# Score matmuls of a causal attention: one pass per head from 64-row operands kept in DRAM by head, in place of four 32-row tiles side by side; constants set up later

## The chip, the cores and the metric

The kernel runs on one core of one Trainium2 chip. The metric is the time of one execution on the device in microseconds (us); the figure for the kernel before is the median of three runs. Durations of single operations come from one profiled execution, whose own time is given beside its span.

## The reference

Two transformer layers over an input of 4 sequences x 2048 tokens x 256 channels, in fp32, each layer an attention and a feed-forward part with a layer norm before and a residual sum behind. Cut to what matters here:

```python
x = x + L0_attn(layernorm(x))      # one head of 64, causal over the 2048 tokens
x = x + L0_ffn(layernorm(x))       # operands rounded to fp8, one 256x256 matmul, bias
x = x + L1_attn(layernorm(x))      # 16 heads of 16, rotary embedding, causal over 2048 tokens
x = x + L1_ffn(layernorm(x))       # token shift mix, sigmoid gate, relu squared

# L1_attn: Q, K, V = x W^T split into 16 heads, rope on Q and K, then per head
scores = Q @ K.T / sqrt(16)
attn = softmax(where(causal, scores, -inf))
out = (attn @ V) @ W_O.T
```

## The kernel before, in words

The tokens are cut into 16 blocks of 512 (`BLK`): 4 sequences (b) with 4 blocks (qb) each. `order` lists them. A block's layer 0 (`l0_attention`, `l0_ffn`), its Q, K, V of layer 1 (`l1_qkv`), its layer-1 attention and what follows (`l1_out`, `l1_ffn`) are separate streams of work.

**A planner sets the order.** Nothing is emitted when the Python code meets it. `op` (L77) and `pe` (L493) record an operation with an engine, an estimated occupancy, the buffers it reads and writes and a stream; `Plan.run` (L118) then lists all operations in the order of a simulated schedule: among the ready ones on each engine it takes the earliest by due time (`key`, L1316), charges TensorE `SWITCH` (L63) for going between its modes (F whole array, R 32-row tiles, C 32-column tiles), and gives buffers of the classes in `CLASSES` (L367) to slots. Each engine executes its list strictly in that order. SP issues the DMAs, also in one order.

**fp32 from fp32r.** Scores are made from an fp32r high part and an fp32r remainder of Q and of K (`split`, L683: a cast on DVE, L686, and a subtraction on GpSimd, L687). All four products (high x high, low x low, high x low, low x high) are summed.

**Q and K of layer 1.** `l1_qkv` projects, applies rope (L862, L866 on GpSimd), splits, and `move` (L691 and L692) copies rows with SP's DMAs into tiles of 128 rows: `k1` and two Q tiles, Qa and Qb, for each of four groups of four heads. A head has 32 rows in each: 8 + 8 high, 8 + 8 low; in Qb high and low change places. So each head's scores are two 32-row matmuls, Qa x K and Qb x K, and four heads lie side by side in the array's four row tiles. Each block takes 48 such moves in layer 1. K and V of all blocks of a sequence stay in SBUF.

**Two phases per group of heads.** Phase D (`d_units`, L906) makes scores with queries on the partitions, only to find each row's maximum: a unit is four heads x 128 queries x up to 512 keys; `d_mm` (L924), on the diagonal block four small matmuls per head that add the causal mask (`d_mask`, L930), then DVE's `reduce_max` (L937). When a group's units are done, `shifts` (L941) negates the maximum (L948), splits it into three bf16 parts on GpSimd (L661 to L664), transposes them on TensorE (L675), and ScalarE copies the rows into M (L679). Phase E (`e_units`, L956) makes scores with keys on the partitions: a unit is four heads x 128 keys x up to 512 queries. `e_shift` (L986) adds the shift by a bf16 matmul of ones with M, `e_mm` (L974) twice, on the diagonal `e_mask` (L980); ScalarE takes the exponent (L993); `values` (L1057) multiplies it with V in four 32-column tiles, fp32.

**The burst.** `burst` (L999) emits the matmuls of two heads of an E unit and two heads of a D unit alternately, so that all four row tiles have work; a second burst has the heads the other way round. If PSUM banks are free in the plan, the first burst also does the shift of the second one's E heads (`ahead`). Each head's scores take one PSUM bank; there are eight. D runs about one group and `LEAD` = 2 units ahead of E (`target`, L1186). Behind every E unit come its values.

**The start.** ScalarE's queue issues loads of constants; GpSimd makes masks, and 48 small DMAs (L461 to L463) copy identity and masks into four-fold form; behind them stand wo0's memset and, on ScalarE's queue, the loads of wo0, bf and wf (L468 to L475); DVE clamps and rounds wf to fp8 values (L476 to L482) before its first layer norm. Block i's x goes to DRAM after layer 0 (`keep_x`) and comes back for Q, K, V and for the end (`fetch_x`).

Layer 0 has one head: its scores are whole-array passes already, 128 rows (64 high, 64 low), L739 and L740 for the maximum, L769 and L770 for the exponent, with the masks L742 and L772.

## Time and profile before

| what | value |
|---|---|
| runs | 2978.33 us median (2966.24 to 2981.45) |
| profiled execution, its own time | 2972.05 us |
| its span, first to last instruction | 2970.2 us |
| granted TensorE clock, mean | 0.971 |
| maxima of phase D, L937 (DVE) | 1425.2 us busy, 2560 of them |
| exponents of phase E, L993 (ScalarE) | 1238.1 us busy, 2560 of them |
| D scores L924, E scores L974 (TensorE) | 944.9 and 874.4 us busy, 5120 of each |
| values L1057 (TensorE) | 613.5 us busy, 5120 of them |
| DMA | 148.54 MB; SP's queue 142.68 MB in 14.6% of 16 engines' time |

How to read it: busy times of lines are unions, and tiles that run side by side are counted in several lines, so they do not add up to the engine's. PE is TensorE's matmuls, PEld its weight loads, which overlap them. A matmul's recorded duration holds its pipeline's latency; what it costs in a stream is the distance from its start to the next start. A timeline line gives the start, the duration from first to last of the merged instructions, engine, line, operation, output and inputs, count, and in brackets how long the engine idled before it and what released it. The lines of the busy times by stretch give the stretch, its length, the busy time of PE, PEld, DVE, ACT and POOL, the granted clock, DMA's busy share and GB/s.

### The profile page before, as it was taken

To read this page: it belongs to the slowest core of one execution; us is meant where nothing else is said; L and a number is where in the kernel's file an instruction comes from. 1 tells how busy PE (TensorE), PEld (TensorE's weight loads), DVE (VectorE), ACT (ScalarE), POOL (GpSimd) and SP (SyncE) were. 2 spreads that over 40 slices of the span, in tenths; PEclk is the share of its full clock that TensorE was granted. 3 is DMA by queue.
4 is the path that set the end of the run, shared out by engine and by line. 5 is a ranking of instruction groups with operands and counts; after the bars stand their busy time and mean duration, and the time that the engine had idled before them with its cause. 6 is when DMAs were issued, how large, how long until landed. Compare 5 with 4: busy or idle time off the path is not lost.

```text
span 2970.2 us, 74535 instructions
## 1 busy us (share of the span) xinstructions
PE 2753.7 (93%) x30485; PEld 1440.9 (49%) x30560; DVE 1935.8 (65%) x3941; ACT 1681.1 (57%) x3441; POOL 721.8 (24%) x983
## 2 busy tenths in 40 slices
PE   2598999999999999999999999999999999999987
PEld 1355545544445555544444555544454565444443
DVE  1256667777663668767773676868685476778771
ACT  1244556656666455655657455565656656566665
POOL 4432313212131132301321141321040323120000
PEclk9699999999999999999999999999999999999998
DMA  2312111210120121211121112121020112010000
GB/s 61 102 54 78 54 37 62 86 40 26 54 69 34 37 80 54 73 37 33 39 77 40 57 55 71 48 68 41 9 79 25 56 59 87 27 43 9 12 12 15
DMA packets 114200, 148.54 MB, mean 50 GB/s; under 512 B 20225, under 2 KB 66754, under 8 KB 113858
## 3 DMA queue, kind: packets, MB, share of 16 engines
q1 hardware_dynamic: 110848, 142.68, 14.6%
q8 instruction: 240, 3.93, 0.5%
q14 instruction: 102, 0.84, 0.1%
q10 hardware_dynamic: 1474, 0.69, 0.1%
q0 software_dynamic: 1536, 0.40, 0.1%
HBM read 63.61 MB, written 16.78 MB: 27 GB/s over the span
## 4 chain that ended last, share of the span: by engine, by line
PE 72%; DVE 11%; POOL 5%; issue 4%; ACT 4%; SPq 2%; DMA 2%; POOLq 0%; ACTq 0%; DVEq 0%
PE ps L1057 16%; PE ps L924 10%; PE ps L623 8%; PE ps L986 8%; PE ps L974 7%; DVE mx L937 6%; PE ps L630 5%; PE ps L781 4%; PE ps L980 3%; PE ps L930 2%; ACT p L993 2%; PE ps L604 2%; SPq L692 2%; PE ps L739 1%; PE ps L769 1%
## 5 line engine op out<-in xcount | busy, mean ns | idle before, releaser
L937 DVE TENSOR_REDUCE mx<-ps 128x1 f32<-128x512 f32 (+3 forms) x2560 | 1425.2, 603 | 615.2 <-PE ps L924 232.4
L993 ACT ACTIVATE p<-ps 128x512 f32<-128x512 f32 (+3 forms) x2560 | 1238.1, 532 | 848.8 <-PE ps L974 340.0
L924 PE MATMUL ps<-k,q 32*128 32x512 f32 (+3 forms) x5120 | 944.9, 422 | 68.7 <-DVE mx L937 40.4
L974 PE MATMUL ps<-q,k 32*128 32x512 f32 (+3 forms) x5120 | 874.4, 433 | 0.3 <-issue 0.3
L1057 PE MATMUL ps<-p,v 128*32 128x512 f32 (+3 forms) x5120 | 613.5, 545 | 1.7 <-issue 1.1
L924 PEld LDWEIGHTS ps<-k,q 32*128 32x128 f32 x5120 | 435.9, 186 | 191.3 <-DVE mx L937 98.0
L986 PE MATMUL ps<-m,ones_b 32*128 32x512 bf16 (+3 forms) x2560 | 455.6, 354 | 14.7 <-ACT p L993 4.8
L974 PEld LDWEIGHTS ps<-q,k 32*128 32x128 f32 x5120 | 419.8, 187 | 80.2 <-issue 77.0
L986 PEld LDWEIGHTS <-ones_b 32*128 32x128 bf16 x2560 | 119.2, 91 | 515.0 <-issue 501.9
L623 PE MATMUL ps<-wb,W 128*128 128x256 f32 x768 | 189.6, 391 | 2.2 <-DVE mx L937 1.6
L661 POOL CAST mp<-sm 128x16 bf16<-128x16 f32 x64 | 17.3, 271 | 704.7 <-DVE sm L948 602.2
L930 PE MATMUL ps<-maskC,identC 32*128 32x32 bf16 (+3 forms) x4096 | 179.9, 201 | 0.0
L1057 PEld LDWEIGHTS ps<-p,v 128*32 128x32 f32 x5120 | 106.0, 108 | 146.7 <-issue 107.9
L980 PE MATMUL ps<-maskTC,identC 32*128 32x32 bf16 (+3 forms) x4096 | 168.3, 197 | 0.0
L623 PEld LDWEIGHTS ps<-wb,W 128*128 128x128 f32 x768 | 139.8, 191 | 32.5 <-issue 8.3
L553 POOL TENSOR_SCALAR sm<-sm 128x4 f32<-128x4 f32 x64 | 14.8, 231 | 576.4 <-DVE sm L547 519.6
L781 PE MATMUL ps<-p,v 128*65 128x512 f32 (+3 forms) x320 | 151.6, 561 | 2.8 <-ACT p L776 2.7
L575 ACT ACTIVATE w<-x,sm 128x256 f32<-128x256 f32 x192 | 105.6, 597 | 60.7 <-DVE sm L560 44.8
L930 PEld LDWEIGHTS <-identC 32*128 32x128 bf16 x4096 | 127.9, 95 | 22.4 <-issue 15.7
L687 POOL TENSOR_TENSOR r<-w,r 128x512 fp32r<-128x512 f32 x80 | 103.5, 1295 | 125.9 <-DVE r L686 77.2
L604 PE MATMUL ps<-ident,w 128*128 128x128 f32 x384 | 66.4, 301 | 72.9 <-ACT w L575 72.1
L630 PE MATMUL ps<-W,wa 128*128 128x512 f32 x256 | 125.4, 617 | 0.7 <-ACT W L608 0.7
(116 smaller groups left out, 2845.6 us busy)
## 6 DMA issues: line engine op xcount, KB each, us to landing
q<-r SPq DMA_DIRECT2D x512, 64.0 KB, 1.9
x<-mid SPq DMA_DIRECT2D x64, 256.0 KB, 3.1
k<-r SPq DMA_DIRECT2D x256, 64.0 KB, 1.9
x<-in_x SPq DMA_DIRECT2D x32, 256.0 KB, 3.8
wa<-in_wqk1T SPq DMA_DIRECT2D x32, 256.0 KB, 2.8
q<-r SPq DMA_DIRECT2D x64, 128.0 KB, 2.4
mid<-x SPq DMA_DIRECT2D x32, 256.0 KB, 2.0
out_y<-x SPq DMA_DIRECT2D x32, 256.0 KB, 2.2
```

The lines of the kernel that those rows point to most:

```text
L604: nc.tensor.transpose(p[:, c0 : c0 + P], T_(src)[:, u * C + k * P : u * C + (k + 1) * P], idn)
L623: nc.tensor.matmul(dst, lhsT[:, k, t * P : (t + 1) * P], w[:, k, :], start=(k == 0), stop=(k == CK - 1),)
L630: nc.tensor.matmul(dst, w[:, k, c0 : c0 + P], xT[:, k, :], start=(k == 0), stop=(k == CK - 1))
L781: nc.tensor.matmul(T_(acc)[: D0 + 1, c0:], T_(V_)[:, kt % TT, :], T_(p)[:, c0:], start=(kt == 0), stop=(kt == nkt - 1),)
L924: nc.tensor.matmul(T_(u.banks[h])[:, : u.w], T_(Q)[ROWS[h], u.t * P : (u.t + 1) * P], T_(u.K)[ROWS[h], : u.w], start=(z == 0), stop=(z == ...
L930: nc.tensor.matmul(T_(u.banks[h])[:, u.w - P + c * 32 : u.w], identC[ROWS[h], c, :], maskC[ROWS[h], c, c * 32 :], start=False, stop=(c == 3),)
L937: op("DVE", dve(u.w), lambda h=h: nc.vector.reduce_max(T_(u.mx)[:, u.t * HG + h, u.kb : u.kb + 1], T_(u.banks[h])[:, : u.w], axis=AX.X), r ...
L974: nc.tensor.matmul(T_(u.banks[h])[:, u.c0 :], T_(u.K)[ROWS[h], k * P : (k + 1) * P], T_(Q)[ROWS[h], u.c0 :], start=False, stop=stop,)
L980: nc.tensor.matmul(T_(u.banks[h])[:, u.c0 : u.c0 + (c + 1) * 32], identC[ROWS[h], c, :], maskTC[ROWS[h], c, : (c + 1) * 32], start=False, ...
L986: nc.tensor.matmul(T_(u.banks[h])[:, u.c0 :], ones_b[ROWS[h], :], T_(u.M)[ROWS[h], u.c0 :], start=start, stop=stop,)
L993: op("ACT", act(u.w), lambda h=h: nc.scalar.activation(T_(u.ps[h])[:, u.c0 :], T_(u.banks[h])[:, u.c0 :], AF.Exp, scale=DK**-0.5), r=[u.ba ...
L1057: nc.tensor.matmul(T_(acc)[h * 32 : (h + 1) * 32, u.c0 :], T_(u.V)[:, u.kt % TT, v0 : v0 + 32], T_(u.ps[h])[:, u.c0 :], start=(u.kt == 0), ...
```

## The change

Q and K of layer 1 are kept in DRAM by head. A head has 64 rows: for K high, high, low, low (16 each), for Q high, low, low, high, so that one matmul of 64 rows sums all four products. `l1_qkv` stores the rope output with 16 DMAs of 256 KB per block; V goes to DRAM through a staging tile. `fetch` brings 64 x 512 operands back: four Q per group, four K per group and key block for D (class `kd`, six slots), four for E (`ke0` to `ke3`, two slots each), and V's part for E.

For E, the operands have 12 more rows (76): in `ke` ones at three rows of the head and zeros elsewhere, set once; in Q the three parts of the shift of all four heads, copied in by one DMA per head after `shifts`. So E is one matmul per head that includes the shift, and on the diagonal one more, of identity and mask, 128 columns (`causal`). D is one matmul per head; its diagonal mask moves to DVE, whose maximum becomes a `tensor_tensor_reduce` with the mask added (`row_max`), in layer 0 too. D and E heads alternate (`both`); values come for two E units at a time (`PAIR`). E starts at the diagonal block. The context goes through DRAM before the output projection.

Constants: the 48 copies are gone; the loads come first; the rest of the memsets, the ones of `ke` and wf's rounding are planned into layer 0 of block 0. Block 0's x is used directly for its Q, K, V. The planner's costs change too.

```diff
+QR = 4 * DK
+SR = 3 * HG
...
-PIPE = {"R": 330.0, "C": 213.0, "F": 200.0}
+PIPE = {"R": 185.0, "C": 213.0, "F": 200.0}
 SLACK_OPT = 250.0
 
-SWITCH = {"RC": 140.0, "RF": 211.0, "CR": 113.0, "CF": 217.0, "FR": 94.0, "FC": 120.0,
-          "RR": -60.0, "FF": 15.0, "CC": 30.0}
+SWITCH = {"RC": 122.0, "RF": 118.0, "CR": 145.0, "CF": 143.0, "FR": 120.0, "FC": 130.0,
+          "RR": -70.0, "FF": 0.0, "CC": 30.0}
...
-                eng_free[e] = s + 60.0
+                eng_free[e] = s + 500.0
...
+OFF_FETCH = -15000.0
+PAIR = 2
...
-        "k1": (16, [P, BLK], F32R),
-        "v1": (4, [P, TT, NH * VW + SLOT_PAD], F32),
-        "q": (10, [P, BLK], F32R),
+
+        "kd": (6, [QR, BLK], F32R),
+        **{f"ke{h}": (2, [QR + SR, BLK], F32R) for h in range(HG)},
+        "q": (10, [QR + SR, BLK], F32R),
+        "v1": (5, [P, TT * HG * VW + SLOT_PAD], F32),
+        "vs": (1, [P, NG, TT * HG * VW], F32),
...
-        "mp1": (2, [P, TT, P], BF16),
-        "m": (2, [P, BLK], BF16),
-        "p": (7, [P, BLK], F32),
+        "mp1": (1, [P, TT, QR + SR], BF16),
+        "m": (1, [P, BLK], F32R),
+        "p": (12, [P, BLK], F32),
...
+    expo = const.tile([P, TT], F32, name="expo")
+    nc.gpsimd.memset(expo, -0.5)
+    warm = const.tile([P, TT], F32, name="warm")
+    nc.scalar.activation(warm, expo, AF.Exp)
+    wo0 = const.tile([D0 + 1, C + 1], F32, name="wo0")
+    nc.gpsimd.memset(wo0, 0.0)
     wqk0 = load([P, CK, 2 * D0], kpn(wqk0T), "wqk0", q=nc.scalar)
     bqk = load([P, 1], bqk0, "bqk", q=nc.scalar)
     wv0 = load([P, CK, D0], kpn(wv0T), "wv0", q=nc.scalar)
     bv_bc = load([P, D0], bv0.partition_broadcast(P), "bv_bc", q=nc.scalar)
+
+    nc.gpsimd.memset(wo0[D0 : D0 + 1, C : C + 1], 1.0)
+    nc.scalar.dma_start(wo0[:D0, :C], wo0T)
+    nc.scalar.dma_start(wo0[D0 : D0 + 1, :C], bo0)
+    wf16 = const.tile([P, CK, C], F16, name="wf16")
+    wcf, wce, wcm = (t[:, :2, :].rearrange("p k n -> p (k n)") for t in tiles["x1"][:3])
+    nc.scalar.dma_start(wcf.rearrange("p (k n) -> p k n", k=CK), kpn(wfT))
+    bf_bc = load([P, C], bf.partition_broadcast(P), "bf_bc", q=nc.scalar)
+    mu_sb = load([P, 2, CK], mu, "mu_sb", q=nc.scalar)
...
+    dmask = const.tile([P, BLK], BF16, name="dmask")
+    nc.gpsimd.memset(dmask, 0.0)
+    nc.gpsimd.affine_select(
+        out=dmask[:, BLK - P :], in_=dmask[:, BLK - P :], pattern=[[-1, P]],
+        compare_op=ALU.is_ge, fill=NEG, base=0, channel_multiplier=1,
+    )
...
-    identC = const.tile([P, 4, P], BF16, name="identC")
-    maskC = const.tile([P, 4, P], BF16, name="maskC")
-    maskTC = const.tile([P, 4, P], BF16, name="maskTC")
-    for h in range(HG):
-        for c in range(4):
-            r, s = slice(h * 32, h * 32 + 32), slice(c * 32, c * 32 + 32)
-            nc.gpsimd.dma_start(identC[r, c, :], ident_b[s, :])
-            nc.gpsimd.dma_start(maskC[r, c, :], mask_b[s, :])
-            nc.gpsimd.dma_start(maskTC[r, c, :], maskT_b[s, :])
...
+    def ready_l0():
+        for t in tiles["v0"]:
+            nc.gpsimd.memset(t[:, :, D0 : D0 + 1], 1.0)
+        for t in tiles["mp0"]:
+            nc.gpsimd.memset(t, 0.0)
+
+    def ready_l1():
+        for t in tiles["mp1"]:
+            nc.gpsimd.memset(t, 0.0)
+        for t in tiles["v1"]:
+            nc.gpsimd.memset(t[:, TT * HG * VW :], 1.0)
+        for t in tiles["vs"]:
+            nc.gpsimd.memset(t, 1.0)
+
+    rows_h = tiles["cx"][0]
+
+    def ready_ke(h):
+
+        r = rows_h[QR : QR + SR, h * P : (h + 1) * P]
+        nc.gpsimd.memset(r, 1.0)
+        nc.gpsimd.affine_select(
+            out=r, in_=r, pattern=[[0, P]], compare_op=ALU.is_ge, fill=0.0,
+            base=-3 * h, channel_multiplier=1,
+        )
+        nc.gpsimd.affine_select(
+            out=r, in_=r, pattern=[[0, P]], compare_op=ALU.is_ge, fill=0.0,
+            base=3 * h + 2, channel_multiplier=-1,
+        )
+        for t in tiles[f"ke{h}"]:
+            nc.gpsimd.tensor_copy(
+                t[QR : QR + SR, :].rearrange("p (a n) -> p a n", n=P),
+                r[:, None, :].to_broadcast([SR, BLK // P, P]),
+            )
+
+    def ready_wf():
+
+
+        nc.vector.tensor_scalar(wcf, wcf, 448.0, -448.0, ALU.min, ALU.max)
+        nc.vector.tensor_scalar(
+            wce.bitcast(I32), wcf.bitcast(I32), 0x7F800000, None, ALU.bitwise_and
+        )
+        nc.vector.tensor_scalar(wcm, wce, 2.0**-6, 1.5 * 2.0**20, ALU.max, ALU.mult)
+        nc.vector.tensor_tensor(wcf, wcf, wcm, ALU.add)
+        nc.vector.tensor_tensor(wf16.rearrange("p k n -> p (k n)"), wcf, wcm, ALU.subtract)
+
+    has = {n: Buf(None, n) for n in ("l0", "l1", "ke", "wf")}
...
+    def row_max(out, sc, w, diag, mx, s):
+
+        def f():
+            a = T_(sc)[:, :w]
+            if diag:
+                nc.vector.tensor_tensor_reduce(
+                    a, a, dmask[:, BLK - w :], 1.0, LOW, ALU.add, ALU.max, out()
+                )
+            else:
+                nc.vector.reduce_max(out(), a, axis=AX.X)
+        op("DVE", dve(w) + (60 if diag else 0), f, r=[sc], w=[mx], stream=s)
+
+    def causal(o):
+
+        nc.tensor.matmul(o, ident_b, maskT_b, start=False, stop=True)
...
-                    nc.tensor.matmul(o[:, :w], T_(Qb)[:, c], Kk[:, :w], start=False, stop=(kb < qb))
-                    if kb == qb:
-                        nc.tensor.matmul(o[:, w - P : w], ident_b, mask_b, start=False, stop=True)
-                pe(f, 2 * w / 2.4 + 20 + (60 if kb == qb else 0), r=[Qa, Qb, k0s[first + kb]],
+                    nc.tensor.matmul(o[:, :w], T_(Qb)[:, c], Kk[:, :w], start=False, stop=True)
+                pe(f, 2 * w / 2.4 + 40, r=[Qa, Qb, k0s[first + kb]],
                    w=[sc, mx], stream=s)
-                op("DVE", dve(w), lambda t=t, kb=kb, w=w, sc=sc: nc.vector.reduce_max(
-                    T_(mx)[:, t, kb : kb + 1], T_(sc)[:, :w], axis=AX.X),
-                   r=[sc], w=[mx], stream=s)
+                row_max(lambda t=t, kb=kb: T_(mx)[:, t, kb : kb + 1], sc, w, kb == qb, mx, s)
...
+        if i == 0:
+            op("DVE", 2700.0, ready_wf, r=[nm], w=[has["wf"]], stream=s)
+            op("POOL", 2500.0, ready_l1, r=[mp], w=[has["l1"]], stream=s)
+            for h in range(HG):
+                op("POOL", 1800.0, lambda h=h: ready_ke(h), r=[mp], w=[has["ke"]], stream=s)
+        M = shift_rows(mp, s, tag, buf("m0", f"m_{tag}"), slice(0, P))
...
+    rot = {n: [Buf(None, f"{n}{i}") for i in range(NBLK)] for n in "kq"}
+    rot_t = {n: [dram.tile([P, 8, BLK], F32, name=f"{n}{i}") for i in range(NBLK)] for n in "kq"}
+    val = [Buf(None, f"v{i}") for i in range(NBLK)]
+    val_t = [dram.tile([P, NG, TT * HG * VW], F32, name=f"v{i}") for i in range(NBLK)]
+
+    def fetch(cls, name, what, i, head, s):
+        b = buf(cls, name)
+        op("SP", 390.0, lambda: nc.sync.dma_start(
+            T_(b)[:QR, :].bitcast(F32),
+            rot_t[what][i][head * 8 : head * 8 + 8].rearrange("d c n -> (d c) n")), r=[rot[what][i]], w=[b], stream=s,
+           off=OFF_FETCH)
+        return b
...
-                for g in range(NG):
-                    for src, part in ((hi, z), (lo, 2 + z)):
-                        dsts = [(Ks[g], part)] if what == "k" else [
-                            (Qas[g], part), (Qbs[g], (part + 2) % 4)]
-                        for dst, pt in dsts:
-                            move(dst, rows(pt), src, rows(g), s, kb=64)
+
+                for src, parts in ((hi, (0, 2) if what == "k" else (0, 3)),
+                                   (lo, (1, 3) if what == "k" else (1, 2))):
+                    for part in parts:
+                        op("SP", 770.0, lambda src=src, r=2 * part + z: nc.sync.dma_start(
+                            rot_t[what][i][:, r, :], T_(src).bitcast(F32)),
+                           r=[src], w=[rot[what][i]], stream=s)
 
         half(C, "k")
         half(0, "q")
         wv1 = load_w(wv1T, 0, s, f"v_{tag}")
+        v = buf("vs", f"v_{i}")
...
+    def d_head(u, h, s):
+
+        def f():
+            nc.tensor.matmul(
+                T_(u.banks[h])[:, : u.w], T_(u.Qs[h])[:QR, u.t * P : (u.t + 1) * P],
+                T_(u.Ks[h])[:QR, : u.w], start=True, stop=True,
+            )
+        o = pe(f, pass_(u.w), r=[u.Qs[h], u.Ks[h]], w=[u.banks[h], u.mx], stream=s)
+        chain(("d", h), o)
+        row_max(lambda: T_(u.mx)[:, u.t * HG + h, u.kb : u.kb + 1], u.banks[h], u.w, u.diag, u.mx, s)
...
+        rows = slice(QR, QR + SR)
+        m = shift_rows(mp, s, tag, buf("m", f"m_{tag}"), rows)
+        for h in range(HG):
+            op("SP", 100.0, lambda h=h: nc.sync.dma_start(
+                T_(u.Qs[h])[rows, :].bitcast(F32), T_(m)[rows, :].bitcast(F32)),
+               r=[m], w=[u.Qs[h]], stream=s)
...
+        kbs = [qb, *range(qb)]
+        for kb in kbs:
+            Ks = [fetch(f"ke{h}", f"ke_{tag}_{kb}_{h}", "k", i - qb + kb, g * HG + h, now[0])
+                  for h in range(HG)]
+            V = buf("v1", f"v1_{tag}_{kb}")
+            op("SP", 500.0, lambda V=V, j=i - qb + kb: nc.sync.dma_start(
+                T_(V)[:, : TT * HG * VW], val_t[j][:, g, :]), r=[val[i - qb + kb]], w=[V],
+               stream=now[0], off=OFF_FETCH)
+            for t in range(TT):
+                u = Unit()
+                u.t, u.diag, u.c0 = t, kb == qb, t * P if kb == qb else 0
+                u.w = BLK - u.c0
+                u.Ks, u.V, u.Qs = Ks, V, Qs
+                u.first, u.last = kb == qb and t == 0, kb == kbs[-1] and t == TT - 1
+                u.banks = [bank(f"e_{tag}_{kb}_{t}_{h}") for h in range(HG)]
+                u.ps = [buf("p", f"p_{tag}_{kb}_{t}_{h}") for h in range(HG)]
+                yield u
...
+    def e_head(u, h, s):
...
+            nc.tensor.matmul(
+                T_(u.banks[h])[:, u.c0 :], T_(u.Ks[h])[:, u.t * P : (u.t + 1) * P],
+                T_(u.Qs[h])[:, u.c0 :], start=True, stop=not u.diag,
+            )
+            if u.diag:
+                causal(T_(u.banks[h])[:, u.c0 : u.c0 + P])
+        o = pe(f, pass_(u.w) + (65.0 if u.diag else 0.0), r=[u.Qs[h], u.Ks[h], has["ke"]], w=[u.banks[h], u.ps[h]], stream=s)
+        chain(("e", h), o)
+        op("ACT", act(u.w), lambda: nc.scalar.activation(
+            T_(u.ps[h])[:, u.c0 :], T_(u.banks[h])[:, u.c0 :], AF.Exp, scale=DK**-0.5),
+           r=[u.banks[h]], w=[u.ps[h]], stream=s)
...
+    def values(us, acc, g, s):
         def f():
+            for u in us:
+                for h in range(HG):
+                    nc.tensor.matmul(
+                        T_(acc)[h * 32 : (h + 1) * 32, u.c0 :],
+                        T_(u.V)[:, (u.t * HG + h) * VW : (u.t * HG + h) * VW + 32],
+                        T_(u.ps[h])[:, u.c0 :], start=u.first, stop=u.last,
+                    )
...
-        qs[i] = l1_qkv(i, fetch_x(i, s, "q"), s)
+        l1_qkv(i, fetch_x(i, s, "q") if i else x, s)
...
+    def both(e, us, s):
+
+        for j in range(HG):
+            if us:
+                d_head(us[0], j, s)
+            if e is not None:
+                e_head(e, j, s)
+        for u in us[1:]:
+            for h in range(HG):
+                d_head(u, h, s)
+        for u in us:
+            if u.last:
+                shifts(u, s)
...
+            for e in e_units(i, g, queries[i, g]):
                 K += 1
...
+                both(e, more_d(K, s), s)
+                wait.append(e)
+                if len(wait) == PAIR or e.last:
+                    values(wait, acc, g, s)
+                    wait = []
...
+        if i + 1 < NBLK:
+            for k in range(CK):
+                op("SP", 1500.0, lambda k=k, cn=cn, i=i: nc.sync.dma_start(con_t[i][k], T_(cn[k])),
+                   r=[cn[k]], w=[con[i][k]], stream=s)
...
-        return w.reshape(NG, HG, 2, DK // 2, C).transpose(4, 2, 1, 3, 0).reshape(C, C)
+        return w.reshape(NH, 2, DK // 2, C).transpose(3, 1, 0, 2).reshape(C, C)
```

## The prediction

> **What bounds the kernel now.** I read the page's busy times first, then the chain of work that ended last, then the busy times by stretch, then stretches of the timeline.
>
> ```profile
> PE 2753.7 (93%) x30485; PEld 1440.9 (49%) x30560; DVE 1935.8 (65%) x3941; ACT 1681.1 (57%) x3441; POOL 721.8 (24%) x983
> ...
> PE 72%; DVE 11%; POOL 5%; issue 4%; ACT 4%; SPq 2%; DMA 2%; POOLq 0%; ACTq 0%; DVEq 0%
> ...
> 0.00:140.40 140.40, 53.96 (x192) 32.36 (x192) 24.69 (x76) 24.42 (x44) 68.20 (x115) 0.78 0.25 79
> 140.40:2895.00 2754.60, 2641.90 (x29726) 1380.45 (x29804) 1899.28 (x3839) 1615.13 (x3308) 646.81 (x859) 0.98 0.15 49
> ```
>
> TensorE (PE) is the bound from 140 us on: 2,642 of 2,755 us. No other engine passes 1,900. In the first 140 us PE idles for 86. So two things are priced: PE's own time in the scores, and the start.
>
> How PE spends a full pair of units (four heads of the exponent phase E, four of the maximum phase D) is read from start times:
>
> ```profile
> 2744.11 1.06 PE L1057 MATMUL ps<-p,v 128*32 128x512 f32 x8
> 2745.11 0.39 PE L986 MATMUL ps<-m,ones_b 32*128 32x512 bf16 x2
> 2745.11 0.49 PE L924 MATMUL ps<-k,q 32*128 32x512 f32 x2
> 2745.14 0.58 PE L974 MATMUL ps<-q,k 32*128 32x512 f32 x2
> 2745.45 0.40 PE L924 MATMUL ps<-k,q 32*128 32x512 f32 x2
> 2745.56 0.40 PE L974 MATMUL ps<-q,k 32*128 32x512 f32 x2
> 2745.89 1.07 PE L1057 MATMUL ps<-p,v 128*32 128x512 f32 x8
> ...
> 2754.75 0.50 PE L974 MATMUL ps<-q,k 32*128 32x512 f32 x2
> ...
> 2755.42 1.99 PE L623 MATMUL ps<-wb,W 128*128 128x256 f32 x8
> ```
>
> A burst with its shift takes 0.78 us, one whose shift was done ahead 0.67: 1.45 for eight heads. Then the values, 1.00 to the next start. All first starts of a burst lie together, so the four tiles do run side by side.
>
> The price of a whole-array pass stands in layer 0, whose scores are already such passes (same fp32r type, 128 rows):
>
> ```profile
> 1526.57 0.23 PE L742 MATMUL ps<-mask_b,ident_b 128*128 128x128 bf16 x1
> 1526.61 0.48 PE L739 MATMUL ps<-k,q 128*128 128x512 f32 x1
> 1526.93 0.40 PE L740 MATMUL ps<-k,q 128*128 128x512 f32 x1
> 1527.16 0.39 PE L739 MATMUL ps<-k,q 128*128 128x512 f32 x1
> 1527.39 0.40 PE L740 MATMUL ps<-k,q 128*128 128x512 f32 x1
> ```
>
> Start to start 0.23 us (median 0.229 over the trace's L739 to L740). After a mask (L742) the next pass takes 0.32 and the mask itself 0.04: together 0.127 more than the pass alone, because a 128-column mask hides little of the next weight load. Narrower passes, by the same rows: 0.173 for 384 columns, 0.117 for 256, 0.113 for 128.
>
> **The scores.** I split PE's time by start-to-start gaps. The 1,087 stretches of score matmuls (L924, L930, L974, L980, L986) last 1,232 us. Taken at the shortest of their kind they are 1,106; the other 126 are waits, mostly for a PSUM bank that VectorE (L937) or ScalarE (L993) still reads. After: 5,120 passes, one per head and phase. Of 640 units, 448 are 512 wide and 64 each 384, 256 and 128; by eight heads that is 3,584 x 0.229 = 821, and 512 x (0.173 + 0.117 + 0.113) = 206. The E masks stay on PE, one for each head of the 256 diagonal units: 1,024 x 0.127 = 130. Sum 1,157. So the passes themselves bring nothing: one pass in place of two or three costs as much when it loses three neighbours. Bounds: a pass between 0.2145 (half of 0.429, the gap of two L630 records, each two streams) and 0.238 (slowest tenth of L740 to L739), -52 to +32; a mask between 0.055 (L675 back to back) and 0.127, -74 to 0. I take the layer-0 rows, the same pair of operations.
>
> **Changes of array shape.** An L630 pass is followed 0.429 us later by another but 0.525 later by a burst: 0.096 for going between 128-row and 32-row tiles; a burst's last pass to values takes 0.32 to 0.33 against 0.229, the same again. Bursts are entered from other whole-array work 616 times; that price goes: -59. Values (32-column tiles) now come for two units at once, so about 308 of 638 leavings go: -30. The price on leaving a burst is inside the 1,106; after, about 320 entries into values remain: +30. Layer 0's maximum phase drops 64 masks: -8.
>
> PE so far: 1,157 + 30 - 1,106 - 59 - 30 - 8 = -16 us. The bulk of the rewrite is a draw on PE.
>
> **What a 64-row pass next to a 76-row pass costs** no row shows: no instruction of this trace has 64 rows, and D (64) and E (76) alternate head by head. Nearest rows: 65-row passes (L790) beside 128-row ones keep their 0.216 gap, price 0; a change to 32-row tiles costs 0.096. A gain is excluded, since no gap goes below the stream. I take 0, by the 65-row row, and keep 0.096.
>
> [...]
>
> **The start.** Before:
>
> ```profile
> 36.82 0.43 DVE L476 TENSOR_SCALAR w<-w 128x512 f32<-128x512 f32 x1 [36.82 <-DMA w<-in_wfT]
> ...
> 44.09 2.17 PE L604 MATMUL ps<-ident,w 128*128 128x128 f32 x8 [44.09 <-ACT w L575]
> ...
> 131.47 4.92 SPq L692 DMA_DIRECT2D q<-r  x8
> ...
> 140.37 1.34 PE L924 MATMUL ps<-k,q 32*128 32x512 f32 x8 [2.58 <-DMA q<-r]
> ```
>
> VectorE stands behind the load of wf, which ScalarE's queue issues only at 33.08, behind POOL's 48 little copies (L461 to L463, 0.5 each, 4.55 to 31.04) and wo0's memset. The copies go and the clamp moves into layer 0. The first x lands about 4.6 us in (issue at 0.72, 3.8 to landing), so the normalization that begins at 39.54 can begin near 8: up to -31. The moved instructions still issue: five for wf on DVE (2.7 us by L476 to L482), memsets and selections on POOL (some 10 us) beside the score phase of block 0, where POOL's next step waits 7 us anyway; if that cover is gone, +10. Block 0 reads x directly: -6.5 (store and load at 86.43 and 88.47). The 48 moves of block 0's Q and K, 0.62 each on SP, last until the first D at 140; 16 stores and 8 fetches replace them, but rope on POOL and a round trip through DRAM (2.0 landing a store, 2.4 a fetch of 128 KB) come next: -5. Not all of this is end time, as block 1 fills some of it: I take -40, bounds -15 to -50.
>
> **Transfers.** Removed: 768 moves (q 512, k 256; 50 MB). Added: 1,536 fetches of 128 KB (201 MB), 256 stores of 256 KB (67), 176 value transfers (31), 256 shift-row copies (6), 60 context copies (16). Traffic goes from 143 to about 415 MB; at the 14.6% of 16 engines that 143 take, 43%. SP issues about 2,680 in place of 1,168, at 0.43 to 0.64 each 1.15 to 1.7 ms, 40 to 58% of the span. It fits, but two waits are new. (1) The row shifts now go by four DMAs (4 x 0.5 issue + 1.9 landing = 4 us) behind the chain maximum, POOL, transpose, ACT (148.54 to about 152): 7.5 us, against the two E units, 5.6 to 8.6 us, that D runs ahead. E's first pass queues behind it, and PE behind that. (2) Six K tiles for D: the third and fourth head's fetch starts only when the first is done, 3 us for a cover of about 3. I take 0.3 us for each of 64 groups and 0.13 for each of 160 key blocks: 40. Bounds 0 and 210 (2 us and 0.5).
>
> **Waits for banks.** Each head now fills and frees one bank by itself, in place of four. I take half of the 126 away: -60; bounds -126 and 0.
>
> **Covered.** Diagonal maxima become two-input operations with the mask: 0.687 (L1165) against 0.682 (L937), at most 0.16 more for the accumulator (as L749): up to 174 us on a VectorE that idles 1,034. If it became late, banks would come late. The extra value copies on ACT (6 us), the context's trip through DRAM and the added ones-rows are hidden behind PE.
>
> **Sum.** -16 - 40 - 60 + 40 = -76 from the profiled 2,972.05 (span 2,970.2): 2,896. The median of the runs shown, 2,978, is 6 higher; I predict **2900**.
>
> **Rivals.**
> - *The array drains between 64 and 76 rows* (ends slower). Place: every D-to-E step in the alternating heads, about 4,700 of 5,120 passes, since some units have no partner. Price 0.096 each: +450, **3350**. It decides from 0.016 us per step, which eats the 76. For it: every shape change seen costs 0.096. Against: 65 rows cost nothing, and the operands start at row 0. This is also the case in which the change does not do what it says.
> - *Transfers take the place of bank waits.* 64 x 2 + 160 x 0.5 = 208 instead of 40: **3064**. For: the shift chain's 7.5 us stand against as little as 5.6. Against: 43% DMA share, and side work for PE between the heads.
> - *PE has it cheaper*: masks at 0.055 (-74), 512-column passes at 0.2145 (-52): **2770**. For: L770 to L772 to L773 in layer 0 stream without such a gap. Against: there a bf16 pass follows the mask, here an fp32r one.
>
> **Chances.** Forecast 0.60 (2820 to 2970), drain 0.16, transfers 0.14, cheaper 0.10. Range 2770 to 3110: it takes in the last two and leaves the drain out. A difference under 0.5% is about what a measurement of this kernel cannot tell from none. Faster by more: 0.54 + 0.10 = 0.64. Same: 0.06 + 0.01 = 0.07. Slower: 0.13 + 0.16 = 0.29.
>
> **What would show it.** D-to-E starts at 0.23 confirm the price; 0.32 is the drain. PE busy near 2,740 with fewer than half the matmuls; first matmul near 12 us, first D near 100. PE idle before an E pass put to the copy into q, or before D to the K fetch, is the second rival. Wrong altogether if VectorE or SP shows over 85% in the middle.

## The result and the profile after

The changed kernel takes **4143.68 us** (median of 4 runs, 4117.62 to 4146.59) against 2979.89 for the kernel before on the same chip: 1.389 times as long, 95% interval 1.382 to 1.397. The forecast was 2900. Times below are medians of runs in the usual state; one run of a later version (values one unit at a time, 3,155 us at a clock of 0.827) fell in a slower one and is left out. The profiled execution took 4144.51 us, span 4142.8, mean granted clock 0.801 (before: 0.971).

The page of the changed kernel: busy times, the clock by slices (tenths of full speed), and the chain of work that ended last.

```profile
PE 4070.0 (98%) x15648; PEld 1985.2 (48%) x15648; DVE 2065.0 (50%) x5029; ACT 1777.5 (43%) x3474; POOL 689.5 (17%) x956
...
PEclk7889687888897778787788788877679876866767
...
PE 96%; issue 1%; DVE 1%; POOL 1%; DMA 1%; ACT 1%; SPq 0%; POOLq 0%; ACTq 0%; DVEq 0%
```

Half as many matmuls keep PE busy 1,316 us longer. The chain is PE and almost nothing else, so no wait for another engine or a transfer has taken the place of the old ones. The clock row is new too: the kernel before ran at 0.98 from 140 us on.

The stretches (PE busy is the second figure, then weight loads, DVE, ACT, POOL, the granted clock, the DMA share and GB/s) show the same state from end to end:

```profile
500.00:1000.00 500.00, 499.82 (x1847) 234.52 (x1846) 264.38 (x611) 224.40 (x423) 83.24 (x112) 0.82 0.32 97
1000.00:2000.00 1000.00, 998.45 (x3952) 491.33 (x3955) 524.64 (x1284) 445.19 (x872) 178.51 (x238) 0.82 0.35 106
2000.00:3000.00 1000.00, 998.54 (x3835) 486.01 (x3828) 505.33 (x1223) 430.12 (x840) 161.36 (x216) 0.80 0.33 99
```

Two pieces of PE's timeline, D (L999, 64 rows) and E (L1051, 76 rows) in turn. First at full clock:

```profile
1049.06 0.50 PE L1051 MATMUL ps<-q,ke 76*128 76x512 f32 x1
1049.49 0.50 PE L999 MATMUL ps<-kd,q 64*128 64x512 f32 x1
1049.92 0.50 PE L1051 MATMUL ps<-q,ke 76*128 76x512 f32 x1
1050.35 0.50 PE L999 MATMUL ps<-kd,q 64*128 64x512 f32 x1
```

then 17 us earlier in the same kernel:

```profile
1031.51 0.80 PE L1051 MATMUL ps<-q,ke 76*128 76x512 f32 x1
1032.24 0.79 PE L999 MATMUL ps<-kd,q 64*128 64x512 f32 x1
1032.99 0.79 PE L1051 MATMUL ps<-q,ke 76*128 76x512 f32 x1
1033.72 0.79 PE L999 MATMUL ps<-kd,q 64*128 64x512 f32 x1
```

Read the starts, not the durations. From start to start it is 0.43 us in the first and 0.73 in the second, where the forecast had 0.229. The stretches that hold them differ in the sixth figure, the clock:

```profile
1021.00:1044.00 23.00, 22.77 (x72) 9.88 (x71) 12.33 (x27) 7.44 (x15) 4.95 (x6) 0.50 0.22 64
1045.00:1057.00 12.00, 12.00 (x40) 6.22 (x37) 5.64 (x9) 8.10 (x15) 2.28 (x2) 1.00 0.43 147
```

**Two losses.** I sorted PE's start-to-start gaps by the granted clock, which in all traces here is 1.0 or 0.5. Where a gap lies at half clock I put the median of the same pair of passes at full clock in its place ("the sum at full clock"):

| kernel | sum of gaps | at full clock | lost to half clock | time spent at half clock |
|---|---|---|---|---|
| before | 2,919 | 2,800 | 119 | 158 |
| changed | 4,127 | 3,256 | 871 | 1,626 |

So 456 us come from longer gaps at full clock and 752 from the clock; about 35 are given back ahead of the first matmul. The steps are counted from the records: 4,067 between a 64-row pass and one of 65 to 128 rows, and 640 into and out of the values' 32-column tiles. How a gap that straddles a change of clock is counted moves such sums by some 20 us.

### The profile page after: what moved, and what is told of

Read it like the earlier page. It is cut to its first block, busy times and chain, and to the rows that moved or that the text cites. A ratio compares the mean times of both kernels' runs of the same rounds, so it can differ in the third digit from the quotient of the medians.

```text
span 4142.8 us, 48929 instructions
## 1 busy us (share of the span) xinstructions
PE 4070.0 (98%) x15648; PEld 1985.2 (48%) x15648; DVE 2065.0 (50%) x5029; ACT 1777.5 (43%) x3474; POOL 689.5 (17%) x956
## 4 chain that ended last, share of the span: by engine, by line
PE 96%; issue 1%; DVE 1%; POOL 1%; DMA 1%; ACT 1%; SPq 0%; POOLq 0%; ACTq 0%; DVEq 0%
PE ps L999 26%; PE ps L1051 25%; PE ps L1067 16%; PE ps L669 8%; PE ps L676 5%; PE ps L850 3%; PE ps L758 2%; PE ps L650 1%; PE ps L807 1%; PE ps L838 1%; PE ps L859 1%; PE ps L808 1%; PE ps L839 1%; PE ps L840 1%; PE ps L1084 1%
## 5 line engine op out<-in xcount | busy, mean ns | idle before, releaser
L1059 ACT ACTIVATE p<-ps 128x512 f32<-128x512 f32 (+3 forms) x2560 | 1314.8, 537 | 1530.3 <-PE ps L1051 918.3
L753 DVE TENSOR_REDUCE mx<-ps 128x1 f32<-128x512 f32 x1632 | 1088.3, 689 | 933.3 <-PE ps L999 893.0
L1051 PE MATMUL ps<-q,ke 76*128 76x512 f32 (+3 forms) x2560 | 1279.5, 525 | 1.8 <-ACT p L1059 1.1
L999 PE MATMUL ps<-kd,q 64*128 64x512 f32 (+3 forms) x2560 | 1254.3, 515 | 7.4 <-issue 3.6
L749 DVE CUSTOM_DVE_ANT_0 ps<-ps,dmask 128x128 f32<-128x128 f32 (+3 forms) x1088 | 533.4, 504 | 719.2 <-PE ps L999 654.1
L999 PEld LDWEIGHTS ps<-kd,q 64*128 64x128 f32 x2560 | 526.7, 212 | 676.2 <-issue 409.1
L1051 PEld LDWEIGHTS ps<-q,ke 76*128 76x128 f32 x2560 | 536.7, 214 | 563.1 <-issue 344.9
L758 PE MATMUL ps<-maskT_b,ident_b 128*128 128x128 bf16 x1088 | 265.3, 246 | 0.0
L758 PEld LDWEIGHTS <-ident_b 128*128 128x128 bf16 x1088 | 114.0, 105 | 96.2 <-issue 49.5
L749 DVE DVE_READ_ACCUMULATOR2_ANT mx<- 128x1 f32 x1088 | 155.1, 143 | 0.0
L845 ACT ACTIVATE p<-ps 128x512 f32<-128x512 f32 (+3 forms) x160 | 85.9, 538 | 99.5 <-PE ps L840 59.9
```

What stands on the lines that cost most here:

```text
L749: nc.vector.tensor_tensor_reduce(a, a, dmask[:, BLK - w :], 1.0, LOW, ALU.add, ALU.max, out())
L753: nc.vector.reduce_max(out(), a, axis=AX.X)
L758: nc.tensor.matmul(o, ident_b, maskT_b, start=False, stop=True)
L845: op("ACT", act(n), lambda c0=c0, sc=sc, p=p: nc.scalar.activation(T_(p)[:, c0:], T_(sc)[:, c0:], AF.Exp, scale=D0**-0.5), r=[sc], w=[p], ...
L999: nc.tensor.matmul(T_(u.banks[h])[:, : u.w], T_(u.Qs[h])[:QR, u.t * P : (u.t + 1) * P], T_(u.Ks[h])[:QR, : u.w], start=True, stop=True,)
L1051: nc.tensor.matmul(T_(u.banks[h])[:, u.c0 :], T_(u.Ks[h])[:, u.t * P : (u.t + 1) * P], T_(u.Qs[h])[:, u.c0 :], start=True, stop=not u.diag,)
```

## The experiments

Theory A: each step between 64 and 76 rows delays the passes around it, and the clock follows from that. Rivals: the steps are not the cause (transfers, banks, the number of passes are); later, several rivals on what moves the clock. Line numbers shift a little from kernel to kernel.

**One change undone: D on 76 rows.** Twelve rows of zeros under the 64, nothing else.

```diff
-        "kd": (6, [QR, BLK], F32R),
+        "kd": (6, [QR + SR, BLK], F32R),      # rows QR.. set to 0.0 once, in q too
-                T_(u.banks[h])[:, : u.w], T_(u.Qs[h])[:QR, u.t * P : (u.t + 1) * P],
-                T_(u.Ks[h])[:QR, : u.w], start=True, stop=True,
+                T_(u.banks[h])[:, : u.w], T_(u.Qs[h])[:, u.t * P : (u.t + 1) * P],
+                T_(u.Ks[h])[:, : u.w], start=True, stop=True,
```

> The passes of D get 76 rows in place of 64 (twelve rows of zeros in K, so the scores are the same); nothing else changes but one setup operation on GpSimd. Theory A (each step between a 64-row pass and any other pass costs about 0.195 us, since the array drains and the next weight load is no longer hidden, and the array that stands idle so often is granted half the clock for 40% of the time): the steps go, D to E starts fall from 0.43 to 0.23 us, the mean granted clock returns from 0.80 to 0.95 or more, and the time falls from 4144 to between 2600 and 2950. Theory B (the steps cost their 0.195, but the clock is low because passes with 64 or 76 of 128 rows count as little work): starts fall to 0.23 but the clock stays near 0.8, 3100 to 3400. Theory C (waits for transfers): nothing moves by over 5%.

2917.52 us (2909.94 to 2921.8), 0.9785 of before, interval 0.9762 to 0.9808. Its page, and its D (L1005) and E (L1057) in turn:

```profile
PE 2779.0 (96%) x15596; PEld 1660.8 (57%) x15648; DVE 1959.8 (67%) x5029; ACT 1674.0 (58%) x3474; POOL 700.8 (24%) x972
...
PEclk8798999999999999999999899999999999999998
```

```profile
1236.33 0.40 PE L1057 MATMUL ps<-q,ke 76*128 76x512 f32 x1
1236.57 0.40 PE L1005 MATMUL ps<-kd,q 76*128 76x512 f32 x1
1236.80 0.40 PE L1057 MATMUL ps<-q,ke 76*128 76x512 f32 x1
1237.04 0.39 PE L1005 MATMUL ps<-kd,q 76*128 76x512 f32 x1
```

0.235 us from start to start in place of 0.43. Twelve rows of zeros are worth 1,226 us, and the rest of the change is faster than before. The sums: 2,764 at full clock (492 less than the changed kernel), 129 lost to the clock (742 less).

**D on 65 rows**, one row of zeros, edited in the same way (`QR + 1`).

> The changed kernel with one row of zeros under the 64 rows of each D pass: 65 rows next to E's 76, all else as it is; the added row adds nothing to any score. [...] Rival B (any two row counts that differ cost something, so 65 next to 76 still pays): 3,300 or more.

2933.0 us, 0.9844 (0.9818 to 0.9871). The D-to-E gap is 0.238 and the sum at full clock 2,757: no step is left. 65 rows beside 76 are free, 64 beside 76 are not: B's 3,300 is out, and the edge lies between 64 and 65 rows.

**Fewer steps: four D heads, then four E heads**, still 64 and 76 rows.

```diff
         for j in range(HG):
             if us:
                 d_head(us[0], j, s)
+        for j in range(HG):
             if e is not None:
                 e_head(e, j, s)
```

> The four D heads of a pair of units are emitted together and then the four E heads, in place of alternately; rows stay 64 and 76. The 4,707 changes of shape between neighbouring matmuls should fall to some 2,000. Theory A: a dose between, 2,700 steps less at 0.195 us (530 us) and a good part of the lost clock: 3000 to 3400, clock 0.88 to 0.97. Theory B: 530 us less and a clock that stays: near 3600. Theory C: no change.

3249.3 us, 1.0901, clock 0.931: 1,726 steps in place of 4,067, and a time between the two. This order shows what one step is made of (512 columns, full clock, medians):

| pair of starts | us | the same with 76 rows |
|---|---|---|
| 64 to 76 | 0.323 | 0.234 |
| 76 to 64 | 0.327 | 0.233 |
| 64 to 64, the first two passes after a step | 0.337 | 0.236 |
| 64 to 64, later | 0.235 | 0.236 |

A step costs 0.09 itself and 0.10 again on the gap behind it, since the second pass after a step starts late too. Where every pass is a step, both fall on every gap: 0.43. Its control is the same order with 76 rows:

> The 76-row version with four D passes and then four E passes, in place of D and E in turn: the control for the grouped version with 64 rows, which took 3,249. Theory A (between 64 and 76 rows the steps cost, the order itself does not): no step is left to save, so 2,917 within 40 us. Rival B (the grouped order costs something of its own, waits for banks by four D passes in a row): 3,000 or more, and the 64-row grouped version's time must be read against that one.

2954.31 us, 0.9925 (0.9902 to 0.9949): the order itself costs 37 us. Against this control the steps of the grouped kernel cost 295.

**E on 64 rows too**: the shift rows and E's causal mask are left out, and the exponent's scale is cut, so this kernel computes another function.

```diff
-                T_(u.banks[h])[:, u.c0 :], T_(u.Ks[h])[:, u.t * P : (u.t + 1) * P],
-                T_(u.Qs[h])[:, u.c0 :], start=True, stop=not u.diag,
+                T_(u.banks[h])[:, u.c0 :], T_(u.Ks[h])[:QR, u.t * P : (u.t + 1) * P],
+                T_(u.Qs[h])[:QR, u.c0 :], start=True, stop=True,
```

> E gets 64 rows like D: its passes leave out the twelve rows of the row shift and the causal mask of E, and the exponent's scale is cut to a thousandth so that it stays finite; so this kernel computes another function. All score passes have 64 rows, and only the steps to other work are left, some 1,500. Theory A: clock 0.93 or more, D to E starts 0.23 us, 2500 to 3000. Theory B (few rows, low clock): the clock stays at 0.8 or falls, 3100 or more. If 64-row passes were slow by themselves, D to E starts would stay above 0.3.

3126.32 us, 1.0488, clock 0.930. The gap of D to E is 0.235, as A had it: two kinds of 64 rows do not step. But the time is above A's range and in B's (3,100 or more), though not with B's clock of 0.8. Its trace has the steps that the expectation counted, 1,515 between 64-row scores and the 128-row side work, whose price A's range left out, and 420 us at half clock though steps are rare.

**The start alone**: the kernel before with the constants set up later, the copies behind, and block 0's x taken directly.

> The kernel before with the later set-up of constants alone: loads first, wf's rounding and the memsets planned into layer 0 of block 0, the 48 small copies issued by SP behind layer 0's maximum in place of GpSimd at the start, and x of block 0 used directly for its Q, K and V. Theory of the prediction: first matmul near 10 us in place of 44, and about 40 us less at the end (15 to 50), 2930 to 2965. Rival: the later work in the first 140 us takes the place of the gap, and the end moves by less than 10 us.

2943.45 us, 0.9866 (0.984 to 0.9891): 36 us, where the forecast had 40.

**What moves the clock.** The steps alone are 492 of the 1,234 us between the 64-row and the 76-row version. For the other 742 I had first "the array streams too few columns". Every D pass issued twice adds columns and no step:

```diff
+            for _ in range(2):
-            nc.tensor.matmul(
+                nc.tensor.matmul(
```

> The changed kernel with every D pass issued twice into the same bank (the second rewrites the same scores): as many steps between 64 and 76 rows as before, but 2,560 passes more, 513 us at full clock (1,792 x 0.229 + 256 x 0.403). Theory A (the granted clock falls because the array, emptied at each step, streams columns for only about half of the time): with more columns streamed between steps the clock comes back to 0.92 or more, and the time is 3,256 (the changed kernel's gaps at full clock) + 513 = 3,770 and up to 4,000 with what is left at half clock: less than the 4,144 of the kernel with half the D passes. Rival B (the clock falls with the amount of work on TensorE, or without regard to it): the clock stays near 0.80 or below and the time is 4,144 + 513 / 0.80 = 4,780 or more.

4856.46 us, clock 0.783. The sum at full clock, 3,779, is what was expected (3,770); the clock got worse, not better (0.801 with D once). More columns alone do not bring it back. The amount of work alone does not lower it either, as the same edit on the 76-row version shows:

> The 76-row version with every D pass issued twice: the added 513 us of passes without the steps. Theory C: the array is in use more than before, the clock stays above 0.96, and the time is 2,917 + 513 = 3,430 or a little less, since the second pass fills waits. Rival B, amount of work: the clock falls as it did when the D passes of 64 rows were doubled (0.80 to 0.78), and the time is above 3,600.

3288.07 us, 1.1059, clock 0.978 against 0.966: the clock stays, and the time is 142 us below the sum of 3,430. Next, "a 64-row pass counts as half": every E pass twice, `stop=n == 0 or not u.diag`.

> The changed kernel with every E pass (76 rows) issued twice into the same bank, the second rewriting the same scores; the D passes (64 rows) once. The same steps between 64 and 76 rows and the same 513 us of added passes as in the version with the D passes twice, which took 4,856 at a granted clock of 0.783; at full clock both come to some 3,780. Theory C (the clock falls when, over about 3.4 us, too little of the array is in use, a 64-row pass counting as half of one: windows of the traces so far with under 3,000 columns so counted fell in 30 to 60% of cases, those over 4,000 in under 5%): the added passes count in full, the clock comes back to 0.90 or more, 3,780 to 4,100. Rival B (the clock falls with the number of steps or the amount of work, whatever kind of pass is added): the clock stays at 0.80 or below, 4,700 or more.

4724.97 us, clock 0.810. That falls as well. Then "the number of steps in a window": D four times, so that steps lie further apart.

> The changed kernel with every D pass issued four times into the same bank: the same steps between 64 and 76 rows, but two of them in 1.55 us in place of 0.86 (one D pass) or 1.08 (two). At full clock 3,778 (the version with two) + 2 x 513 = 4,805. Theory D (the granted clock falls with the number of steps in a window of 3.4 us: in the traces so far 8 and more steps were followed by a fall in over 90% of windows, 6 and 7 in 27 to 65%, 4 and 5 in 4 to 10%, 3 or fewer in under 2%): 4.4 steps in a window, so the clock comes back to 0.90 or more and the time is 4,850 to 5,300, about that of the version with half as many D passes (4,856). Rival B (the clock falls with steps of any density once work stands between them, or with the work of 64-row passes): the clock stays at 0.78 to 0.80 and the time is 6,000 or more.

6278.66 us, and the lowest clock of all, 0.759. The page of this kernel:

```profile
PE 6242.4 (99%) x23259; PEld 3588.3 (57%) x23328; DVE 2113.4 (33%) x5029; ACT 1785.3 (28%) x3474; POOL 687.2 (11%) x956
...
PEclk6877787776888777877679778786678875776667
```

By the profile TensorE was never busier (99%), and its clock never lower. What survived came from cutting nine traces into windows of 3.41 us (the clock's stretches are multiples of that) and asking of each window at full clock whether the next is at half. The measure that sorts them is the **cells in use**: for each pass that starts in the window, streamed columns x rows/128 x weight columns/128, the columns counted once, as the record gives them. A window holds some 8,150 columns (512 in 0.2145 us, half of the 0.429 of an L630 pass; one expectation writes 8,192). Windows followed by half clock, of all at full clock:

| kernel | under 2,500 | to 3,000 | to 3,500 | above |
|---|---|---|---|---|
| before | 14 of 31 | 3 of 35 | 1 of 117 | 0 of 620 |
| changed | 112 of 169 | 37 of 168 | 4 of 198 | 0 of 189 |
| D twice | 73 of 119 | 84 of 220 | 17 of 244 | 0 of 217 |
| D four times | 32 of 48 | 105 of 243 | 44 of 372 | 0 of 286 |
| 76 rows | 18 of 29 | 5 of 41 | 0 of 98 | 0 of 614 |

In this measure a 64-row pass counts 0.5, a 76-row pass 0.59, and of each gap of 0.43 us only 0.2145 streams: D and E in turn come to 8 x 512 x (0.5 + 0.594) / 2 = 2,240. More 64-row passes (D four times) leave a window under 3,500 too. That was read off traces, so it was tested: 52 rows of zeros under E's 76, with D left at 64. Steps, passes and columns stay; only cells are added.

```diff
-        "q": (10, [QR + SR, BLK], F32R),      # ke alike
+        "q": (10, [P, BLK], F32R),            # rows QR.. set to 0.0 once
```

> The changed kernel with 52 rows of zeros under the 76 rows of both operands of every E pass (128 rows), D still at 64: the same steps, passes and streamed columns; the zeros add nothing to any score. Theory F (the clock is granted by the cells of the array in use, rows x columns x streamed columns, in a window of 3.4 us: over nine traces no window above 3,500 of 8,192 full columns was followed by a fall, those from 2,500 to 3,000 in 7 to 45% and those below in 25 to 63%): a window of nothing but D and E in turn goes from 8 x 512 x (0.5 + 0.594) / 2 = 2,240 to 8 x 512 x (0.5 + 1) / 2 = 3,070, so most falls go, the clock comes to 0.92 or more and the time from 4,144 to between 3,300 and 3,600; the steps stay, with gaps of 0.43. Rival B (the clock follows the steps themselves, or zeros do not count): 4,144 within 60.

3763.5 us, 1.2619 (1.2557 to 1.2681). The page, then one stretch:

```profile
PE 3700.4 (98%) x15648; PEld 1843.0 (49%) x15648; DVE 2059.0 (54%) x5029; ACT 1775.0 (47%) x3474; POOL 697.1 (18%) x974
...
PEclk7789999989898889897999888989889997888878
```

```profile
1000.00:2000.00 1000.00, 998.50 (x4349) 496.40 (x4341) 545.45 (x1352) 493.80 (x968) 174.63 (x242) 0.92 0.37 111
```

380 us saved by multiplying zeros: the time at half clock goes from 1,626 to 798 us, at the same 4,707 changes of shape and the same gap of 0.43 (0.92 against 0.82 in the clock of this stretch). Windows with six or seven steps are followed by half clock 11 times in 217, where the changed kernel has 49 in 184. The direction is the theory's, the size half of it: 3,300 to 3,600 was expected. A window of D and E alone now holds some 3,070 cells, still on the slope (24 of 290 between 3,000 and 3,500; 0 of 423 above).

Then zeros to row 127 under everything, no step left:

> The 76-row version with zeros down to row 127 in both operands of all D and E passes: no step, the same passes. Theory F: its 199 us at half clock were windows with few cells in use; those in the middle of the kernel go, those at the start stay, the clock goes from 0.966 to 0.975 or more and the time from 2,917 to between 2,840 and 2,890. Rival B (zeros do not count): 2,917 within 15.

**2881.09 us** (2875.68 to 2882.04), 0.9674 of before, interval 0.9645 to 0.9702: the fastest version here, faster than the kernel before and than the 76-row version. The page and the same stretch:

```profile
PE 2741.6 (95%) x15648; PEld 1640.0 (57%) x15648; DVE 1958.9 (68%) x5029; ACT 1672.1 (58%) x3474; POOL 704.1 (24%) x980
...
PEclk6799999999999999999999999999999999999998
```

```profile
1000.00:2000.00 1000.00, 981.53 (x5711) 592.27 (x5711) 734.08 (x1872) 606.52 (x1259) 257.26 (x342) 1.00 0.53 155
```

105 us at half clock are left, against 199 with 76 rows. Over the eight traces that were not used to find the measure, no window above 3,500 was followed by half clock (0 of 4,785); under 2,500 it was 146 of 231.

This table counts a pass's columns once, but an fp32 pass of the values or the side work takes as long as two streams (L630: 0.429 for 512 columns, against 0.23 for a score pass; L623 of the kernel before, 256 columns: 0.216 in fp32, 0.109 in fp16). Counted twice, the same measure sorts the windows of all 17 traces more sharply: 356 of 378 under 2,500 are followed by half clock, 487 of 714 up to 3,000, 188 of 1,065 up to 3,500 and 10 of 11,651 above. At equal cells it matters little whether the kernel has steps between 64 and more rows: from 3,000 to 3,500 it is 154 of 872 windows in the seven kernels with such steps and 34 of 193 in the ten without, from 2,500 to 3,000 it is 428 of 618 and 59 of 96. So, as far as these windows show, the steps lower the clock mainly by leaving few cells in a window.

**Values: one, two or three units at a time**, all on the 76-row version, then three on 128 rows.

```diff
-PAIR = 2
+PAIR = 1
```

> The 76-row version with the values taken for each unit by itself in place of two at once: some 310 more entries into the 32-column tiles of the values and as many more leavings, the term of the sum that was put at 30 us each way. By that term, 0.096 for each of 620 changes: 60 us more, 2,977. By the larger price that the steps between 64 and 76 rows showed (0.195): 120 us more, 3,040. If values' passes hide their own changes: 2,917 within 15.

3017.06 us (2990.64 to 3025.34), 1.0116 (1.0057 to 1.0174): some 100 more than two at a time (the next expectation writes 3,021 and 104). The sum at full clock grows by 49, 0.077 for each of 638 more changes of shape, near the 0.096 that the forecast used; the rest is clock again (325 us at half in place of 199).

> The 76-row version with the values taken for three units at once instead of two (16 tiles for the exponents in place of 12, eight work tiles in place of ten). One unit at a time cost 104 us more than two (3,021 against 2,917) with 638 more changes of array shape: 0.16 each, clock included. Three at a time saves about 100 entries and as many leavings: 200 x 0.16 = 32 us, 2,885. If fewer work tiles hold up the side work, or the longer run of values lets VectorE and ScalarE run dry, it is 2,917 or more.

2970.16 us, 0.9974 (0.9956 to 0.9992): slower than two at a time. With 297 us at half clock the clock was suspected:

> The same 128 rows with the values for three units at once. With 76 rows three at once took 2,970, 53 more than two, though its gaps at full clock sum to 10 us less; 297 us of it were at half clock against 199. Theory F: with 128 rows the half-clock time goes and three at once is level with two or up to 15 us faster, 2,830 to 2,890. Rival (three at once is slower by waits for work tiles): 30 us or more above the version with two.

2916.92 us, 0.9799 (0.9771 to 0.9826): most of the half-clock time goes (137 us are left), but it stays 36 us behind two at a time. So it was not the clock alone: by the same sums some 16 of the 36 are there at full clock too. Whether the two fewer work tiles or the longer run of values costs the 36 was not tried.

## Why the prediction was wrong, step by step

**The step that failed** is "What a 64-row pass next to a 76-row pass costs": "I take 0, by the 65-row row, and keep 0.096". The 65-row row was right about 65 rows, and says nothing about 64: the cost begins between the two (0.43 and 0.238 beside 76), and 64 beside 64 is free (0.235). Why the edge lies there was not shown, nor that the array drains at a step; the traces show late starts. In the alternation above the weight load of the D pass starts with the pass itself (both at 1049.49, with no load running for the 0.25 before), where in a run of one shape it starts a pass ahead (L739 in the kernel before: load at 1526.93, pass at 1527.16). Measured, a step is 0.195 for each pass of a strict alternation, so D to E starts lay at 0.43, beyond even the 0.32 that was to show the drain.

The upper bound, 0.096, was half of that, because only the gap at the change was read. The other half, the late start of the second pass, stood in the kernel before as well:

```profile
2067.73 1.06 PE L1057 MATMUL ps<-p,v 128*32 128x512 f32 x8
2068.73 0.50 PE L769 MATMUL ps<-q,k 128*128 128x512 f32 x1
2069.07 0.40 PE L770 MATMUL ps<-q,k 128*128 128x512 f32 x1
2069.30 0.39 PE L773 MATMUL ps<-m,ones_b 128*128 128x512 bf16 x1
```

The first whole-array pass behind the values takes 0.34 to the next start, the second 0.23. At full clock the first gap behind a 32-row or 32-column pass has a median of 0.337 for L739 to L740 (40 of them) against 0.23 in a run, 0.533 for L630 to L630 (72) against 0.429, and 0.321 for L790 to L790 (41) against 0.217: 0.10 more each time. Over all 4,067 steps the price is 492 / 4,067 = 0.12, because many stand where the 76-row version has longer gaps anyway (its 512-column D passes have a median of 0.31 to the next start, not 0.23).

**The drain rival** had the place right and nearly the net sum, 450 against 492, but by luck. Its 4,700 steps between D and E are 2,608 in the trace, or 3,300 with those that have E's mask between them; only with the steps to side work are there 4,067. And it set half the price of an alternating step; the mean came down to 0.12 because many steps stand at gaps that are long anyway. Yet 3,350 is 794 below the measurement. **The clock** is the second step that failed, a term put at nothing without a reason: no case of the forecast priced it, and each took the 0.98 of the kernel before for granted. 742 of the 1,234 us, three fifths, come from that. The traces show two states (1.0 and 0.5), in stretches of 3.41 us and multiples of it, and a busy TensorE is not spared: the changed kernel's, 98% busy, was at half clock for 1,626 us, and with D four times, 99% busy, the clock was 0.759. What went with the falls is few cells in use (112 of 169 windows under 2,500 in the changed kernel, 0 of 189 above 3,500).

The rest can be judged from the 76-row version, 2,917 against the 2,900 forecast:

- **Start**: first matmul at 9.7 us (forecast near 12), first D at 98.0 (near 100), both in the changed kernel; alone 36 us (40). Right.
- **Passes**: 0.233 to 0.236 for 0.229. Right for a pass inside a run. Of the 112 pairs L739 to L740, whose median the forecast gave as 0.229, that holds for the 38 behind another L740; the median of all is 0.32, as the others follow a mask or a change of shape. **Masks**: with 0.239 ahead of it and 0.040 behind, a mask adds 0.044 to a pass, not 0.127: the lower bound, 0.055, was nearer.
- **Changes of shape with the values**: 320 entries are left, as forecast.
- **Waits for banks**: "I take half of the 126 away: -60" is not what the sum of gaps shows: those behind score matmuls come to 1,460 us against 1,232 before. Waits for banks need not be what grew: PE's idle time ahead of score passes that the profile puts to maxima (L937, then L754 and L758) or exponents (L993, then L1065) fell from 66 to 18 us. The values went from 579 to 533, and all other work on TensorE from 1,108 to 900, where some 60 had been priced. The parts are off by some 200 us each way and cancel: -26 in all. What moved from the side work into the scores stays open.
- **Transfers**: 417 MB (about 415), 48.1% of the 16 engines in the 76-row version (43%), and in the changed kernel PE waits 1.2 us for q and not at all for K, as it is late itself. In the 76-row version PE's waits for them, with the reason's total, count and longest:

```profile
PE ps L1005 <- DMA q<-q: 10.1, 16, 1.8
PE ps L1005 <- DMA kd<-k: 7.3, 13, 1.3
...
PE ps L1057 <- DMA q<-m: 1.5, 2, 1.3
```

  19 us for the 40 forecast; the rival of 3064 is out.
- **Covered**: the added accumulators on VectorE cost 155 us (up to 174) and hide: VectorE is 50% busy in the changed kernel, 67% in the 76-row one. The group, with its count, busy time and mean in ns:

```profile
L749 DVE DVE_READ_ACCUMULATOR2_ANT mx<- 128x1 f32 x1088 | 155.1, 143 | 0.0
```

So 2900 was close to what the change gives once the step is gone, partly by errors that cancel; as a forecast of this kernel it failed on one price and on a clock that was taken as fixed.

## What to carry to other kernels

Before two kinds of matmul alternate, compare their rows, and try the smaller padded with zeros: here each step between 64 and 76 rows delayed two starts, by 0.09 and 0.10 us, and with 65 or 76 beside 76 none was late. With fp32r and 128 weight columns the zeros cost no time on TensorE (0.235 us a pass with 76 rows and with 128). Read the granted clock with every gap, and estimate the cells in use for the new mix as well as the time: a price in microseconds at full clock was two fifths of this loss. And a nearest row is near only if it lies on the same side of the edge, here between 64 and 65 rows.

## What the runs showed of the hardware that was not expected

- 64 and 65 rows are different things beside 76: 0.43 and 0.238 us per pass.
- A step between 64 and 76 rows delays two starts, by 0.09 and 0.10 us; behind 32-row and 32-column passes the second start is 0.10 late too.
- The clock was never halved after a window of 3.41 us with over 3,500 of some 8,150 columns' worth of cells in use (0 of 8,401 windows in 17 traces, an fp32 pass's columns counted once); under 2,500 it was in 490 of 822, or in 356 of 378 with these columns counted twice. Zeros count as use: rows of zeros alone took the time at half clock from 1,626 to 798 us.
- More work can go with a lower clock: 64-row passes issued four times over gave 0.759 with PE 99% busy, issued once 0.801 with 98%.
- Still open: what brings the clock back. In the changed kernel, windows at half clock with three or more steps were almost never followed by full clock (2 of 266), but no one measure sorted these windows as the cells sort the falls.
